# One routed row for all six ranks: layer 0's rows carry six table rows, weights and destinations, and each page finds its own

## The chip, the cores and the metric

The kernel runs on one core of one Trainium2 chip. A core has TensorE (PE, matmuls, with its weight loads shown apart as PEld), VectorE (DVE), ScalarE (ACT), GpSimd (POOL) and SyncE (SP), and 16 DMA engines. DMAs are issued by SP and ACT (plain ones) and by POOL (indirect ones, whose addresses come from a tile of row numbers). The metric is the device time of one execution in microseconds (us). Before the change it was 2058.91 us, the median of 3 runs (2055.96 to 2059.22).

## The reference

The input is x with 128 graphs of 64 nodes and 256 features, so 8192 tokens, and an adjacency matrix for each graph. Two layers follow each other. Each layer is a graph part and a mixture of experts, both added to their input:

```
# layer 0
x = x + graph0(layernorm(x), adj)       # aggregate, 256 -> 1024, rms norm, silu, 1024 -> 256
x = x + experts0(layernorm(x))          # 64 experts of 256 x 256, the 6 best for each token
# layer 1
x = x + graph1(layernorm(x), adj)
x = x + experts1(layernorm(x))          # 8 experts 256 -> 512 -> 256, the 2 best for each token

def experts0(x):
    top, which = top_k(x @ gate_w.T, 6)
    p = softmax(top)                                    # six weights for a token
    y = sum_k p[k] * (x @ lattice_weights[which[k]])    # six products for a token
    return layernorm(x + y @ out_w.T + out_b) * ln_g + ln_b
```

The change is in experts0: how the six copies of a token get to their experts, and how each copy's weight and place of return travel with it.

## The kernel before, in words

The work has four stages, one behind the other.

The block stage of layer 0 (about 0 to 600 us) takes 32 blocks of 256 tokens. A block goes through the graph part, is normalized (`residual_b`, L729), transposed (`turn`, L741), gated (`gate`), and its six best experts are found (`choose`). `count` and `places` work out where each of the six copies of a token goes in a table in DRAM, which has one row for a copy and is filled by expert, so that each 128 rows in it (a page) belong to one expert. `send` (L776, L330) then writes the rows with indirect DMAs on POOL's queue: one for each of two tiles and six ranks of a block, 12 in all, each with 128 rows. `staggered` runs the stages of several blocks side by side with the lags of the list at its end: `place` is 3 blocks behind, the sends of the ranks 2 to 5 are 4 behind.

A row has 258 columns: 256 of the token, one with the destination (token x 6 + rank, an integer in a float's bits), one with the weight. As destination and weight differ between the ranks, the tile xs holds six copies of a block's tokens: ACT writes them with one ACTIVATE of 1536 columns for each of two tiles (L736), `weigh` (L278) writes the destinations, `release` (L303) the weight of one rank before its sends.

The lattice stage (about 613 to 1177 us) first takes 12 early pages, the first page of each of 12 experts, and then 404 pages in 202 pairs (`mean_pages`; more only if the routing needs them, and here it does not). A pair goes through `fetch` (SP reads two pages into a tile px, 22 buffers, asked for 12 pairs ahead), `flip` (PE transposes, ACT copies), and `apply` (L907): PE multiplies each page by its expert's matrix, DVE scales the result by the weight column of px into px itself (L922), and `reply` (L339) writes the 128 results with an indirect DMA on POOL's queue to the rows of `r0.answer` that the destination column of px names. A page table, made by DVE at the end of the block stage (`page_table`, L358), tells which rows and which expert a page has. Rows of a page that no token fills come from a filler tile; its destination is out of range, so that nothing is written for it. During the first 64 pairs ACT also issues a fill of the end of an expert's part of the table.

The graph stage of layer 1 (from 1131 us on, beside the end of the lattice stage) begins with `load_y`, which reads the six products of each token from `r0.answer`. The first five blocks may be read before the last replies land, the others wait for them. The expert stage of layer 1 (about 1530 us to the end) is the same idea with other sizes and is not touched, but shares the class `Router`.

On PE, DVE and ACT the instructions run in the order in which the program writes them (`manual_schedule`). On SP and POOL a planner orders them. All waits are put in by the framework: whoever writes a tile's buffer again waits until those that used the buffer before are done with it. A tile has as many buffers as its `bufs` says, or else its pool; the pool `wx0` of the lattice stage has three:

```
with tc.tile_pool(name="wx0", bufs=3, reuse_waits="tile") as wx, \
...
stages = ((-12, fetch), (0, apply),
          (-2, lambda j: flip(j) if j < 4 else None), (-3, lambda j: flip(j) if j >= 4 else None))
```

The numbers are lags: in step s the kernel writes fetch of pair s+12, apply of pair s, and flip of pair s+3.

Of the kernel before, what the change touches and what calls it, by code (L numbers as in the profile page):

```python
# [78 lines left out]
class Router:  # L79
# [14 lines left out]

    def __init__(self, tc, pool, small, dram, n, D, E, K, T, pg, S, epoch, name, R, total=None, like=None):
        nc = tc.nc
# [9 lines left out]
        self.spare = self.chunks * self.pitch  # L106
        self.W = D + 2
        assert T == 2 and epoch == 4 and n % self.EP == 0 and S % pg == 0 and (5 * T * P <= S or S >= n)
# [30 lines left out]
        nc.gpsimd.memset(self.filler, 0.0)  # L139
        fill_to = self.filler[:, :, D].bitcast(I32)  # L140
        if total is None:
            self.answer = dram.tile([n * K, D], F32, name=name + "y")
            nc.gpsimd.iota(fill_to, pattern=[[0, pg // P]], base=n * K, channel_multiplier=0)
        else:
            nc.gpsimd.iota(fill_to, pattern=[[P, pg // P]], base=n, channel_multiplier=1)
            nc.sync.dma_start(out=total[n:n + pg, :].rearrange("(t p) d -> p t d", p=P), in_=self.filler[:, :, :D])
# [4 lines left out]
    def look(self, m):  # L151
# [10 lines left out]
        v.memset(self.firsts, 0.0)  # L162
        v.tensor_scalar(self.firsts[:, :m], t, float(self.spare), None, op0=ALU.add)
        self.full_pages -= m

# [112 lines left out]
    def weigh(self, b, top, xs):  # L278

        nc, T, K, D, n = self.nc, self.T, self.K, self.D, self.name  # L280
        w = self.small.tile([P, T, K], F32, name=n + "w")
        den = self.small.tile([P, T], F32, name=n + "den")
        nc.vector.tensor_scalar(xs[:, :, :, D].bitcast(I32), self.dest, float(b * T * P * self.each), None,
                                op0=ALU.add)
        nc.vector.tensor_sub(w, top[:, :, :K], top[:, :, 0:1].to_broadcast([P, T, K]))
        nc.scalar.activation(w, w, AF.Exp)
        return w, den
# [9 lines left out]

    def normalize(self, w, den):
        nc = self.nc
        nc.vector.reduce_sum(den, w, axis=AX.X)  # L300
        nc.vector.reciprocal(den, den)

    def release(self, k, w, den, xs):  # L303

        self.nc.vector.tensor_mul(xs[:, :, k, self.D + 1], w[:, :, k], den)

    def places(self, b, hot):

# [13 lines left out]
        prod = self.work.tile([P, T, K, E], F32, name=n + "prod", bufs=1)  # L322
        nc.vector.tensor_mul(prod, hot, place.unsqueeze(2).to_broadcast([P, T, K, E]))
        row = self.small.tile([P, T, K], F32, name=n + "rowf")
        nc.vector.tensor_reduce(row, prod, op=ALU.add, axis=AX.X)
        out = self.small.tile([P, T, K], I32, name=n + "row")
        nc.vector.tensor_copy(out, row)
        return out

    def send(self, row, xs, late, ranks=None, tiles=None):  # L330
        groups = ("late", "send") if late else ("send", "late")
        for t in tiles or range(self.T):
            for k in ranks or range(self.K):
                i = self.nc.gpsimd.indirect_dma_start(  # L334
                    out=self.table[:, :], out_offset=bass.IndirectOffsetOnAxis(ap=row[:, t, k:k + 1], axis=0),
                    in_=xs[:, t, k, :], in_offset=None)
                self.alone(i.ins, *groups)

    def reply(self, i, x, y):  # L339

        d = self.nc.gpsimd.indirect_dma_start(  # L341
            out=self.answer[:, :],
            out_offset=bass.IndirectOffsetOnAxis(ap=x[:, self.D:self.D + 1].bitcast(I32), axis=0),
            in_=y, in_offset=None, bounds_check=self.n * self.K - 1, oob_is_err=False)
# [13 lines left out]
    def page_table(self, scratch):  # L358
# [83 lines left out]
        v.tensor_scalar(self.tab[:, 0, :], row, float(self.spare), None, op0=ALU.add)  # L442
        v.tensor_scalar(self.tab[:, 1, :], exp, float(E - 1), None, op0=ALU.min)

    def fill_end(self, e):
# [49 lines left out]
def two_layer_gnn_moe_kernel(ctx: ExitStack, tc: tile.TileContext, a: dict, out: bass.AP):  # L495
# [83 lines left out]
    xn1_dram = [dram.tile([C, D], F32, name=f"xn1_{b}") for b in range(NB)]  # L579
    r0 = Router(tc, const, small, dram, N, D, E0, K0, T, P, 14 * P, 4, "r0", 3)  # L580
    W = r0.W
    r1 = Router(tc, const, small, dram, N, D, E1, 2, T, 2 * P, N, 4, "r1", 1, total=out, like=r0)

    lat_pool = tc.tile_pool(name="lat", bufs=1)
# [19 lines left out]
    with tc.tile_pool(name="c0", bufs=1) as c0, \  # L604
# [124 lines left out]
        def residual_b(b):  # L729
# [3 lines left out]
            nc.vector.scalar_tensor_tensor(nm, mv[:, :, 0], -1.0, rs, op0=ALU.mult, op1=ALU.mult)  # L733
            B["xs"] = xs = work.tile([P, T, K0, W], F32, name="xs", bufs=3)
            for t in range(T):
                nc.scalar.activation(xs[:, t, :, :D], x1[:, t, :].unsqueeze(1).to_broadcast([P, K0, D]),  # L736
                                     AF.Identity, bias=nm[:, t:t + 1], scale=rs[:, t:t + 1])
            nc.sync.dma_start(out=by_tile(x1_dram[b]), in_=x1)
            nc.sync.dma_start(out=by_tile(xn1_dram[b]), in_=xs[:, :, 0, :D])

        def turn(b):  # L741
            B = blocks[b]
            pt = psum.tile([P, KD, C], F32, name="ps")
            ops.transpose(pt, B["xs"][:, :, 0, :])
            B["xn1T"] = xn1T = work.tile([P, KD, C], F32, name="xn1T", bufs=1)
# [20 lines left out]
        def place(b):  # L766
            B = blocks[b]
            r0.normalize(*B["w"])
            B["row"] = r0.places(b, B["hot"])
            send(b, 0)  # L770
# [5 lines left out]
        def send(b, k):  # L776

            B = blocks[b]
            r0.release(k, *B["w"], B["xs"])
            r0.send(B["row"], B["xs"], b > LOOK, (k,))  # L780
# [55 lines left out]
    with tc.tile_pool(name="e0", bufs=1, reuse_waits="tile") as ex, \  # L836
# [6 lines left out]
        for j in (0, 3, 2, 1, None, 4, 5):  # L843
            if j is None:
                ex.tile([P, 1008], F32, name="space")
            else:
                early[j] = ex.tile([P, 2, W], F32, name=f"early{j}")
        xTs = {}
# [14 lines left out]
        def apply_early(j):  # L863
            py = py_pool.tile([P, 2, D], F32, name="py")
            for q in range(2):
                for k in range(KD):
                    nc.tensor.matmul(py[:, q, :], lhsT=xTs[j][:, k, ts(q, P)], rhs=lat[:, 2 * j + q, k, :],
                                     start=(k == 0), stop=(k == KD - 1))
            for q in range(2):
                px = early[j][:, q, :]  # L870
                nc.vector.tensor_scalar(px[:, :D], py[:, q, :], px[:, D + 1:D + 2], None, op0=ALU.mult)
                r0.reply(0, px, px[:, :D])

# [5 lines left out]
    with tc.tile_pool(name="wx0", bufs=3, reuse_waits="tile") as wx, \  # L879
# [7 lines left out]
        def fetch(j):  # L887
            Q = pairs[j]
            Q["px"] = px = wx.tile([P, 2, W], F32, name="px", bufs=22)
            for q in range(2):  # L890
# [6 lines left out]
        def flip(j):  # L897
# [7 lines left out]
            nc.scalar.copy(xT[:, :, :n * P], pt[:, :, :n * P])  # L905

        def apply(j):  # L907
            Q = pairs[j]
# [12 lines left out]
            for q in range(n):  # L921
                nc.vector.tensor_scalar(px[:, q, :D], py[:, q, :], px[:, q, D + 1:D + 2], None, op0=ALU.mult)  # L922
                r0.reply(2 * j + q, px[:, q, :], px[:, q, :D])


        stages = ((-12, fetch), (0, apply),
                  (-2, lambda j: flip(j) if j < 4 else None), (-3, lambda j: flip(j) if j >= 4 else None))
# [19 lines left out]
    with tc.tile_pool(name="c3", bufs=1, reuse_waits="tile") as c3, \  # L947
# [146 lines left out]
        def residual1_b(b):  # L1094
            B = blocks[b]
            rs, nm = ops.scale_shift(B["mv3"], B["std3"])
            B["xs"] = xs = work.tile([P, T, 2, W], F32, name="xs", bufs=3)
            for t in range(T):
# [72 lines left out]
    with tc.tile_pool(name="pt4", bufs=2, space=PSUM, reuse_waits="tile") as pt_pool, \  # L1171
# [15 lines left out]
        def fetch1(i):  # L1187
            Q = pages[i]
            Q["x"] = x = wx.tile([P, 2, W], F32, name="px", bufs=4)
            if i < 0:  # L1190
# [88 lines left out]
```

## Time and profile before

| | |
|---|---|
| median of 3 runs | 2058.91 us (2055.96 to 2059.22) |
| the profiled execution | 2052.92 us, span of its instructions 2051.1 us |
| granted TensorE clock, mean | 0.974 |
| busy over the span: PE, DVE, POOL, ACT | 1923.0, 1200.0, 1162.0, 1018.1 us |
| POOL's indirect DMAs: sends, early replies, replies | 384, 12, 404 |
| replies, mean of one | 973 ns busy, 123.3 us idle before all of them |
| sends, mean of one | 1047 ns busy |
| HBM | 195 GB/s over the span |

A line of a group has the line of the code, the engine, the operation, the tiles written and read, the shape and the count; then busy us, the mean ns of one, and the idle time of the engine before them with what ended it. A line of the order of time has its start in us, its length, the engine and the line; a bracket at its end tells how long the engine sat idle before it and what it was waiting for. A view of one tile has min/median/max in ns and the first and last start in us. Busy times are shares of a span whose stages have different limits; the stretches of the prediction take them apart.

### The profile page before, as it was taken

The numbers are of one execution on the slowest core, as the hardware profiler recorded it, in microseconds if no ns is written. First come the engines' busy times: TensorE is split into PE (matmuls) and PEld (weight loads), VectorE is DVE, ScalarE is ACT, GpSimd is POOL, SyncE is SP. The second block draws the span as 40 slices with busy tenths as digits, with TensorE's granted clock in tenths as the row PEclk, the third lists the DMA queues.
The fourth block names the chain that finished last, engine by engine and source line by source line (L and its number), as shares of the span: only waits on it lengthen the run. The fifth ranks groups of instructions, "written<-read, shape, count | busy, mean of one in ns | idle before, by whom it ended". The sixth has DMA issues, their size and how long they took to land. (4 is left out here: it accounts for less than half of the span.)

```text
span 2051.1 us, 37214 instructions
## 1 busy us (share of the span) xinstructions
PE 1923.0 (94%) x10516; PEld 1678.1 (82%) x10516; DVE 1200.0 (59%) x4205; ACT 1018.1 (50%) x2033; POOL 1162.0 (57%) x1134
## 2 busy tenths in 40 slices
PE   6999999999966989999999799999989999999996
PEld 5888888888865778888877688888868888888885
DVE  5899999999975333344333389999862222222221
ACT  4888888888851222222222266666643333333332
POOL 1377667677677777777777723333343444444443
PEclk9999999999977999999999899999989999999998
DMA  4244555544476988666665799888527766666664
GB/s 123 80 143 148 168 165 170 169 159 141 133 267 206 309 252 267 214 207 207 207 207 171 266 362 338 267 278 278 190 92 172 178 162 162 162 163 163 163 163 86
DMA packets 282561, 397.91 MB, mean 194 GB/s; under 512 B 56025, under 2 KB 236393, under 8 KB 282353
## 3 DMA queue, kind: packets, MB, share of 16 engines
q1 hardware_dynamic: 202880, 246.61, 40.2%
q0 software_dynamic: 64416, 136.14, 22.1%
q10 hardware_dynamic: 15056, 12.69, 1.9%
q8 instruction: 94, 1.54, 0.3%
q14 instruction: 115, 0.93, 0.2%
HBM read 222.84 MB, written 176.64 MB: 195 GB/s over the span
## 5 line engine op out<-in xcount | busy, mean ns | idle before, releaser
L334 POOL DMA_INDIRECT r0x<-xs,r0row x384 | 402.1, 1047 | 236.0 <-DVE lat L706 72.2
L341 POOL DMA_INDIRECT r0y<-px x404 | 393.3, 973 | 123.3 <-DMA r0y<-px 49.7
L918 PE MATMUL py<-lat,pxT 128*128 x1616 | 389.4, 384 | 18.7 <-ACT pxT L905 15.4
L351 POOL DMA_INDIRECT out_x<-py_s,px x138 | 214.6, 1555 | 293.8 <-DMA out_x<-py_s,px 125.9
L922 DVE TENSOR_SCALAR px<-py,px 128x256 f32<-128x256 f32 x404 | 177.0, 480 | 309.6 <-PE py L918 303.9
L918 PEld LDWEIGHTS py<-lat,pxT 128*128 128x128 f32 x1616 | 294.3, 192 | 59.3 <-ACT pxT L905 20.4
L905 ACT COPY pxT<-pt 128x512 f32<-128x512 f32 x202 | 117.9, 585 | 368.6 <-PE pt L903 252.7
L1217 ACT ACTIVATE phid<-ph,pw 128x256 f32<-128x256 f32 x276 | 130.6, 473 | 323.2 <-issue 213.9
L1215 PE MATMUL ph<-pxT,pw 128*128 128x256 f32 x1104 | 251.3, 381 | 0.7 <-ACT pxT L1206 0.7
L1235 PE MATMUL py<-fw,phid 128*128 (+1 forms) x1104 | 249.7, 379 | 0.0
L717 PE MATMUL ps<-lat 128*128 128x256 f32 x1024 | 238.5, 382 | 0.0
L1215 PEld LDWEIGHTS ph<-pxT,pw 128*128 128x128 f32 x1104 | 210.9, 191 | 30.0 <-ACT pxT L1206 1.1
L684 PE MATMUL ph<-lat 128*128 128x256 f32 x1024 | 232.2, 386 | 2.7 <-DVE lat L706 2.0
L1235 PEld LDWEIGHTS py<-fw,phid 128*128 128x128 f32 x1104 | 204.5, 190 | 25.0
L684 PEld LDWEIGHTS ph<-lat 128*128 128x128 f32 x1024 | 195.1, 193 | 29.4 <-issue 2.4
L334 POOL DMA_INDIRECT r1x<-xs,r1row x128 | 127.7, 998 | 160.9 <-DVE r1run L313 47.0
L717 PEld LDWEIGHTS ps<-lat 128*128 128x128 f32 x1024 | 193.8, 192 | 24.9
L1229 DVE TENSOR_SCALAR p<-p 128x2 f32<-128x2 f32 x69 | 12.8, 186 | 225.5 <-ACT p L1228 225.5
L1238 DVE TENSOR_TENSOR py_s<-py,pb 128x512 f32<-128x512 f32 x69 | 47.7, 692 | 154.9 <-PE py L1235 152.7
L903 PE MATMUL pt<-ident,px 128*128 128x128 f32 x808 | 125.3, 276 | 11.6 <-DMA px<-r0x 11.3
L903 PEld LDWEIGHTS pt<-ident,px 128*128 128x128 f32 x808 | 100.4, 142 | 37.7 <-DMA px<-r0x 8.9
L994 PE MATMUL ps<-ident,y 128*128 128x128 f32 x768 | 94.7, 281 | 16.1 <-DMA y<-r0y 16.1
(303 smaller groups left out, 2980.4 us busy)
## 6 DMA issues: line engine op xcount, KB each, us to landing
px<-r0x SPq DMA_DIRECT2D x404, 129.0 KB
y<-r0y SPq DMA_DIRECT2D x64, 768.0 KB
pw<-in_L_ffn_W1b SPq DMA_DIRECT2D x69, 514.0 KB
px<-r1x SPq DMA_DIRECT2D x69, 258.0 KB
x<-x SPq DMA_DIRECT2D x64, 256.0 KB
pb<-in_L_ffn_b SPq DMA_DIRECT2D x69, 128.0 KB
r0x<-r0filler ACTq DMA_DIRECT2D x64, 129.0 KB
lat<-in_x SPq DMA_DIRECT2D x32, 256.0 KB
```

Source lines behind the costliest of these rows:

```text
L334: i = self.nc.gpsimd.indirect_dma_start(out=self.table[:, :], out_offset=bass.IndirectOffsetOnAxis(ap=row[:, t, k:k + 1], axis=0), in_=xs[ ...
L341: d = self.nc.gpsimd.indirect_dma_start(out=self.answer[:, :], out_offset=bass.IndirectOffsetOnAxis(ap=x[:, self.D:self.D + 1].bitcast(I32 ...
L351: i, d = f"{self.name}add{i}", self.nc.gpsimd.indirect_dma_start(out=self.total[:, :], out_offset=bass.IndirectOffsetOnAxis(ap=x[:, self.D ...
L684: nc.tensor.matmul(ph[:, c, :], lhsT=w1[:, k, ts(2 * j + c, P)], rhs=B["aggT"][:, k, :], start=(k == 0), stop=(k == KD - 1))
L717: nc.tensor.matmul(B["po"][:, t, :], lhsT=B["hT"][:, c, ts(t, P)], rhs=w2[:, c, :], start=False, stop=(t == T - 1 and c == KH - 1))
L903: nc.tensor.transpose(pt[:, k, ts(q, P)], Q["px"][:, q, ts(k, P)], ident)
L905: nc.scalar.copy(xT[:, :, :n * P], pt[:, :, :n * P])
L918: nc.tensor.matmul(py[:, q, :], lhsT=xT[:, k, ts(q, P)], rhs=lat[:, ds(regs["e"][(2 * j + q) % 4], 1), k, :].rearrange("p o d -> p (o d)") ...
L922: nc.vector.tensor_scalar(px[:, q, :D], py[:, q, :], px[:, q, D + 1:D + 2], None, op0=ALU.mult)
L1215: nc.tensor.matmul(ph, lhsT=w[:, k * F1 + c * P:k * F1 + (c + 1) * P], rhs=Q["xT"][:, k, :], start=(k == 0), stop=(k == KD - 1))
L1217: nc.scalar.activation(hid[:, c, :], ph, AF.Relu, bias=w[:, KD * F1 + c:KD * F1 + c + 1], scale=1.0)
L1235: nc.tensor.matmul(py[:, t, :], lhsT=Q["hid"][:, c, ts(t, P)], rhs=fw2[:, ds(e, 1), c, :].rearrange("p o d -> p (o d)"), start=(c == 0), s ...
```

## The change

Each token of a block has one row for all six ranks. The row has 274 columns: 256 of the token, six table rows (where each of the six copies stands), six weights, six destinations. `xs` has one copy of the tokens in place of six and four buffers in place of three; every send of a block reads the same row. `places` writes the six table rows into `xs` as floats, `normalize` writes all six weights at once, and `release` turns one rank's table rows into integers for the send's addresses, where it wrote one rank's weights before.

A page no longer finds a weight and a destination at a fixed column. The new function `own` compares the six table rows of each row of a page with the row's own place in the table, and sums weights and destinations over the one rank where they are equal. It has four DVE instructions for a pair and writes four small tiles, the last of which, `to`, holds the integers that the reply's indirect DMA takes as its addresses. For that a page must know its own rows: `page_table` writes the first rows of all pages to DRAM, and `spread_rows` reads them back to all 128 partitions and adds the partition's number. In the list of stages `own` of pair s+1 is written ahead of `apply` of pair s. px has 20 buffers in place of 22. The early pages call `own` in `apply_early`, with tiles in the pool `et`, which has four buffers.

```diff
-        self.W = D + 2
+        self.W = D + (3 * K if shared else 2)
...
     def page_table(self, scratch):
...
+        if self.shared:
+            v.tensor_scalar(row, row, float(self.spare), None, op0=ALU.add)
+            nc.sync.dma_start(out=self.rows_dram, in_=row)
+
+    def spread_rows(self, pool):
+
+        n = -(-self.pages // 4) * 4
+        out = pool.tile([P, n], F32, name=self.name + "rows", bufs=1)
+        flat = self.rows_dram.rearrange("p j -> (p j)")[:n]
+        self.nc.sync.dma_start(out=out, in_=rows_of(flat))
+        self.nc.vector.tensor_scalar(out, out, self.lane, None, op0=ALU.add)
+        return out
...
     def weigh(self, b, top, xs):
-        nc.vector.tensor_scalar(xs[:, :, :, D].bitcast(I32), self.dest, float(b * T * P * self.each), None,
+        nc.vector.tensor_scalar(xs[:, :, D + 2 * K:], self.dest, float((b * T * P - self.n) * self.each), None,
                                 op0=ALU.add)
...
-    def normalize(self, w, den):
+    def normalize(self, w, den, xs):
...
+        nc.vector.tensor_mul(xs[:, :, D + K:D + 2 * K], w, den.unsqueeze(2).to_broadcast([P, self.T, K]))
+
+    def release(self, k, row, xs):
+
+        self.nc.vector.tensor_copy(row[:, :, k], xs[:, :, self.D + k])
+
+    def own(self, px, rows, small):
+
+        v, D, K = self.nc.vector, self.D, self.K
+        n = px.shape[1]
+        mine = small.tile([P, 2, K], F32, name=self.name + "mine")[:, :n]
+        got = small.tile([P, 2, 2, K], F32, name=self.name + "got")[:, :n]
+        out = small.tile([P, 2, 2], F32, name=self.name + "sum")[:, :n]
+        to = small.tile([P, 2], I32, name=self.name + "to")[:, :n]
+        v.tensor_tensor(mine, px[:, :, D:D + K], rows.unsqueeze(2).to_broadcast([P, n, K]), op=ALU.is_equal)
+        v.tensor_mul(got, px[:, :, D + K:].rearrange("p q (a k) -> p q a k", k=K),
+                     mine.unsqueeze(2).to_broadcast([P, n, 2, K]))
+        v.tensor_reduce(out, got, op=ALU.add, axis=AX.X)
+        v.tensor_scalar(to, out[:, :, 1], float(self.n * K), None, op0=ALU.add)
+        return out[:, :, 0], to
...
     def places(self, b, hot, xs=None):
+        if xs is not None:
+            nc.vector.tensor_reduce(xs[:, :, self.D:self.D + K], prod, op=ALU.add, axis=AX.X)
+            return out
...
-    def reply(self, i, x, y):
+    def reply(self, i, to, y):
-            out_offset=bass.IndirectOffsetOnAxis(ap=x[:, self.D:self.D + 1].bitcast(I32), axis=0),
+            out_offset=bass.IndirectOffsetOnAxis(ap=to, axis=0),
...
-            B["xs"] = xs = work.tile([P, T, K0, W], F32, name="xs", bufs=3)
+            B["xs"] = xs = work.tile([P, T, W0], F32, name="xs", bufs=4)
             for t in range(T):
-                nc.scalar.activation(xs[:, t, :, :D], x1[:, t, :].unsqueeze(1).to_broadcast([P, K0, D]),
-                                     AF.Identity, bias=nm[:, t:t + 1], scale=rs[:, t:t + 1])
+                nc.scalar.activation(xs[:, t, :D], x1[:, t, :], AF.Identity, bias=nm[:, t:t + 1], scale=rs[:, t:t + 1])
...
-            Q["px"] = px = wx.tile([P, 2, W], F32, name="px", bufs=22)
+            Q["px"] = px = wx.tile([P, 2, W0], F32, name="px", bufs=20)
...
+        def own(j):
+            n = min(2, r0.pages - 2 * j)
+            pairs[j]["own"] = r0.own(pairs[j]["px"][:, :n], page_rows[:, 2 * j:2 * j + n], wx)
...
-                nc.vector.tensor_scalar(px[:, q, :D], py[:, q, :], px[:, q, D + 1:D + 2], None, op0=ALU.mult)
-                r0.reply(2 * j + q, px[:, q, :], px[:, q, :D])
-        stages = ((-12, fetch), (0, apply),
+                nc.vector.tensor_scalar(px[:, q, :D], py[:, q, :], Q["own"][0][:, q:q + 1], None, op0=ALU.mult)
+                r0.reply(2 * j + q, Q["own"][1][:, q:q + 1], px[:, q, :D])
+        page_rows = r0.spread_rows(wx)
+        stages = ((-12, fetch), (-1, own), (0, apply),
```

## The prediction, before the change was run

> **What bounds the kernel now.** I read the stretches by engine first, then the reply tile's own instructions, then the order of time at three places. Columns of the stretches: length, busy time of PE, weight load, DVE, ACT, POOL (instructions), granted clock, DMA share, GB/s.
>
> ```profile
> 100.00:550.00 450.00, 440.42 (x2486) 387.04 (x2485) 426.10 (x1438) 380.34 (x728) 316.43 (x302) 1.00 0.47 156
> 590.00:660.00 70.00, 40.36 (x187) 32.50 (x186) 44.07 (x159) 11.91 (x19) 53.84 (x54) 0.73 0.70 228
> 660.00:800.00 140.00, 125.54 (x661) 106.62 (x660) 48.19 (x110) 32.27 (x56) 106.44 (x111) 0.99 0.91 279
> 800.00:1000.00 200.00, 198.82 (x1101) 174.96 (x1101) 80.47 (x184) 53.90 (x93) 152.12 (x157) 1.00 0.70 215
> 1000.00:1130.00 130.00, 121.43 (x623) 100.22 (x621) 45.69 (x105) 29.60 (x51) 98.96 (x102) 0.99 0.63 190
> ```
>
> In the block stage (to about 590) PE is busy 98% and DVE 95%. In the lattice stage (660 to 1130) PE looks like the bound, but POOL only looks free: 0.97 of DMA_INDIRECT plus 0.30 of issue is a 1.275 us beat without a hole, 157 in 200 us. The replies' own rows tell who ends last:
>
> ```profile
> L341 POOL DMA_INDIRECT r0y<-px x404: 967/969/1412, 660.8 to 1176.0; - x135
> L341 POOL DMA_INDIRECT r0y<-early x12: 969/972/992, 645.5 to 659.5; - x12
> ```
>
> 404 replies at 1.275 are 515 us, which is 660.8 to 1176.0: POOL sets the end of this stage, 2.55 us a pair of pages, where an unstalled PE takes 2.17. PE's and DVE's lead over it is stored in the 22 buffers of px:
>
> ```profile
> 1130.09 0.97 POOL L341 DMA_INDIRECT r0y<-px  x1 [0.30 <-DMA r0y<-px]
> 1130.39 0.88 DVE L922 TENSOR_SCALAR px<-py,px 128x256 f32<-128x256 f32 x2 [0.85 <-PE py L918]
> ```
>
> DVE finishes the last pair at 1131.3, POOL 46 us (18 pairs) later. PE spends that time on the next stage. Two stretches show what it gets done:
>
> ```profile
> 1131.00:1152.00 21.00, 8.98 (x46) 8.40 (x47) 0.59 (x4) 0.58 (x1) 15.81 (x18) 0.70 0.92 317
> 1152.00:1190.00 38.00, 34.43 (x217) 30.12 (x216) 25.62 (x91) 19.38 (x42) 20.15 (x22) 0.98 0.72 272
> ```
>
> 21 us are start-up (constants and first loads), then PE is nearly full. Last, what a tile costs that a reply still reads:
>
> ```profile
> 654.44 0.97 POOL L341 DMA_INDIRECT r0y<-early  x1 [0.30 <-DMA px<-r0x]
> ...
> 659.60 1.07 ACT L905 COPY pxT<-pt 128x512 f32<-128x512 f32 x2 [2.99 <-DMA r0y<-early]
> ```
>
> ACT wants memory of a tile that a reply reads, and starts 5.2 us after that reply's issue: the tile is held until the data has landed, not until POOL has issued. The landing records of the 404 replies, counted from the end of POOL's 0.97, have these medians: 3.2 us for the first 120 replies, 1.9 for the next 248 (quartiles 1.6 and 2.3), 4.9 for the last, when the next stage's constants load.
>
> **The change, part by part.** The sum is made on the profiled execution: 2052.9 us (span 2051.1); the median of the timed runs, 2058.9, is 6 higher.
>
> *Routed row without six copies.* Per block ACT writes two times 256 columns in place of 1536:
>
> ```profile
> L736 ACT ACTIVATE xs<-x,bn_nm,rstd x64: 1652/1677/1687, 54.4 to 604.9; 128x1536 f32<-128x1536 f32 x64
> L708 ACT ACTIVATE lat<-lat,c_L_gnn_rms_weight 128x256 f32<-128x256 f32 x211 | 87.1, 494 | 3.5 <-DVE lat L706 3.2
> L76 PE MATMUL ps<-ident,xs 128*128 128x128 f32 x108 | 17.5, 285 | 9.6 <-ACT lat L677 9.6
> ```
>
> 2 x (1.677 - 0.494) = 2.4 us of ACT a block, 76 in all, but beside a PE that is 98% busy. What PE can gain is its wait behind ACT's queue in front of the turn (L76): 9.6 us over 27 blocks. DVE at 95% may keep half. Taken: -5, ends -10 and 0. After 588 POOL sends without a hole until 645, so the shorter ACT chain of the last blocks gains nothing there. The wait for a free xs buffer is 0.2 us in all, so the fourth buffer is worth nothing.
>
> *DVE in the block stage.* weigh, release and places keep their counts; one 12-element product comes in (0.165, as L285), one cast goes (0.173, L327): 0. One operation more in look, one in the page table, and a few constants at the start: under 1 us, beside POOL's sends and the first loads.
>
> *Rows of 1096 bytes in place of 1032.* Sends, fetches and fills move 6% more, 7 MB in all. POOL's issue time does not follow the size (0.969 median for sends and replies), SP issues the same number of fetches, and the fetches are far ahead: 0, but it lengthens landings a little; that is inside the bounds below.
>
> *Page rows.* One store and one spread load on SP behind the page table, whose last operation is at 637.2, then one DVE operation ahead of the first own. The first scale of the stage now is at 655.6, and POOL needs it only at 660.8 (early replies before it). If SP put the store ahead of the six lattice loads that it issues from 571 to 600, 6 MB at 0.3 MB/us would end at 657: still covered to within some 5 us. If the spread load fell behind the first 40 page fetches (58 in 41.6 us, so 29 us after 646.7), scale and POOL would start 16 us late. Taken 0, ends 0 and +16.
>
> *own: the added work.* Four small DVE operations a pair (0.157 to 0.186 each by L300, L285, L1229), 0.66 x 202 = 133 us on an engine that is 40% busy in this stage: hidden as work. POOL's descriptor work can suffer from it: a send takes 1.051 on average beside a DVE busy 95%, a reply 0.973 beside 40%. 25 points more DVE make 0.078 x 25/55 = 0.035 a reply at most in proportion, x 404 = 14; many of the block stage's operations are long, so I take +8, ends 0 and 32 (all 0.078).
>
> The Trainium skill (SBUF — State Buffer, Who interferes with whom) states that a DVE instruction with two SBUF inputs contends with a GpSimd instruction that reads SBUF, the second to issue blocking fully. If each of own's two such products held up a reply for its 0.16 us, that would be 65 us instead of 8; the row of the sends, under a far denser DVE, speaks against it.
>
> *own: the added wait.* This is the term that decides. `to` has three buffers (the pool's default). So own(j+1) writes the tile that reply(j-2) reads, and must wait until it has landed. On DVE own(j+1) stands ahead of the scales of pair j, behind which wait reply(j) on POOL and, four py buffers on, PE's matmuls. DVE loses its lead: two pairs instead of 18. And a loop closes: second reply of j-2 issued, 0.97 + landing L, `to` 0.19, first scale 0.48, POOL's start after DVE 0.27 (L305 ends 551.90, send 552.17), reply(j) issued, 1.275 on to its second. Two pairs then take 3.2 + L, against 5.1 now: it costs as soon as L is over 1.9, the very median of the middle of the stage.
> First 64 pairs, where the fills run too: L 3.2 gives 3.2 a pair, +42; a slower loop moves less, so I take L 2.8, +29. The other 138: only the landings over 1.9 count, about 0.2 a time, 0.1 a pair, +14. Sum +43; ends 0 (L never over 1.9) and +100 (all landings as recorded, the last 16 pairs' too).
>
> The Trainium skill (DMA: Bandwidth & Descriptors, Anatomy of one DMA — SWDGE (gpsimd) path) puts a software DMA's fixed time at about 2 us, most of it the write receipt. An estimate by that page, L 2.0 throughout, would make +10 instead of +43; the records of this trace go above it wherever loads compete.
>
> *The lost lead.* PE's last matmul now comes about 11 us before the last reply, not 46. Then start-up 21 us (with 9 us of work) and the other 34.4 us of work at full rate: PE reaches the state of 1190 (13 us after the last reply now) some 45 us after it. Cost 32; ends 25 (start-up quicker without the replies' traffic) and 46 (the whole lead). The two px buffers fewer cost nothing once the lead is two pairs.
>
> Sum: -5 + 8 + 43 + 32 = +78, so 2131 on the profiled execution and 2137 on the median. I say 2135, its own range 2095 to 2180.
>
> **The rivals.**
> *Held only until issue.* If `to` is free when POOL has read the offsets, the loop is 3.2 us for two pairs and never binds; only the lead goes: -5 + 8 + 32 = +35, about 2091. Against it: ACT's wait above, which is for a landing; for it: that tile held data, not offsets.
> *Faster: the wait does not bind DVE at all.* If the tile is released so that DVE may run ahead as now, own is hidden, POOL's beat and end stay, and the block stage's L76 wait decides: -10 + 0 to +5, about 2052 on the median. It decides only if DVE's lead stays above some 15 pairs. Three buffers speak against it.
> *Landings grow.* If fetches and fills bunch up so that L stays at 4.1 (the 90% point of the first 120 replies), a pair takes 3.65: +1.1 x 202 = 222, with the lead some 2310.
>
> **How the numbers follow.** Forecast 0.72, held until issue 0.11, faster 0.11, landings grow 0.06. Slower is the first, second and fourth. Of the faster case 0.02 lies within 0.2% (4 us, about what a measurement of this kernel tells from none). Below 2070 lie 0.11 of the chance, above 2185 some 0.08; so the range is 2070 to 2185.
>
> **What would show it.** DVE's own line in the lattice stage waits for DMA r0y<-px, some 200 times. POOL's replies show holes and end near 1220 instead of 1177; DVE's last scale is within 6 us of that end. The xs activation falls to about 0.5 us. The share of DMA in the stage falls. The prediction is wrong if POOL's beat stays at 1.275 and DVE still ends 40 us ahead of it, or if the spread load holds up the first pair.

## The result, and the profile after

The changed kernel takes 2184.93 us (median of 4 runs, 2177.05 to 2190.62); the kernel before, beside it, 2059.06 (2055.96 to 2059.88). The ratio is 1.061, with an interval of 1.057 to 1.065: slower by 126 us, where the forecast was slower by 76. The profiled execution took 2188.7 us, with a span of 2186.9; before it was 2051.1, so the two profiles differ by 135.8.

Where the 135.8 lie, from the start times of the same instructions in both traces (all in us from the start; "lead" is the time from the end of DVE's last scale to the end of POOL's last reply; the block period is the mean over the blocks 8 to 28, and replies are counted from start to start):

| | before | after | difference | forecast for this piece |
|---|---|---|---|---|
| block period | 17.93 | 18.29 | +0.36 a block | |
| last send of the block stage | 644.2 | 656.6 | +12.4 | -5 |
| from there to the first reply of a page | 16.6 | 29.8 | +13.2 | 0 (end +16) |
| first to last reply (404) | 515.1 | 585.9 | +70.8 | +43 and +8 |
| lead | 45.8 | 3.9 | | |
| last reply to the end | 875.1 | 914.6 | +39.5 | +32 |

All four pieces grew. I go through them, the lattice stage with its lead first.

**The lattice stage.** Stretches by engine of the kernel after (length, busy time of PE, weight load, DVE, ACT, POOL with instructions, granted clock, DMA share, GB/s):

```profile
100.00:550.00 450.00, 443.96 (x2448) 384.69 (x2448) 427.57 (x1417) 321.19 (x717) 318.23 (x295) 1.00 0.49 158
660.00:800.00 140.00, 109.42 (x523) 90.45 (x524) 57.76 (x246) 25.66 (x44) 78.59 (x82) 0.91 0.77 235
800.00:1000.00 200.00, 162.59 (x826) 135.85 (x825) 95.72 (x414) 39.69 (x68) 132.97 (x138) 0.97 0.68 207
```

Between 800 and 1000 POOL issued 157 indirect DMAs before and 138 now; PE fell from 198.8 to 162.6 us. No engine is full any more: something that is not an engine sets the pace. The waits name it (engine, line, what it waited for: total us, times, longest):

```profile
DVE r0to L331 <- DMA r0y<-px,r0to: 288.1, 166, 4.5
...
POOL r0y L371 <- DVE px L968: 109.1, 140, 8.9
PE py L964 <- DVE r0mine L327: 93.9, 99, 2.9
```

DVE waits 166 times for a reply to land before it may write the next destinations (L331, `to`), POOL waits behind DVE, and PE behind DVE. In the order of time, at the end of the stage (start, duration, engine, line; in brackets the idle time before it and what ended it):

```profile
1267.67 0.17 DVE L331 TENSOR_SCALAR r0to<-r0sum 128x2 int32<-128x2 f32 x1 [2.51 <-DMA r0y<-px,r0to]
1267.75 1.65 DVE L968 TENSOR_SCALAR px<-py,r0sum 128x256 f32<-128x256 f32 x4
1268.50 0.98 POOL L371 DMA_INDIRECT r0y<-px,r0to  x1 [1.73 <-DVE px L968]
...
1272.34 0.97 POOL L371 DMA_INDIRECT r0y<-px,r0to  x1 [0.30 <-issue]
```

The landing ends 2.51 us of idleness on DVE, then come `to`, the scales, and POOL's reply, which had been waiting 1.73 us. The last four replies follow at 1.28 us each. The replies' own rows, and the scales':

```profile
L371 POOL DMA_INDIRECT r0y<-px,r0to x404: 966/969/986, 686.4 to 1272.3; - x135
```

```profile
L968 DVE TENSOR_SCALAR px<-py,r0sum x404: 466/476/484, 685.7 to 1268.9; 128x256 f32<-128x256 f32 x135
```

A reply is as long as before (0.969 median); only the holes between the replies are new. The last scale now starts 3.4 us before the last reply, not 45.

**From the last send to the first reply.** SyncE's queue from 640 to 700, and then the order of time there, after:

```profile
SPq L518 <- DMA r0x<-xs,r0row: 34.2, 4, 30.5
SPq L522 <- DMA r0y<-early,r0to: 9.1, 1, 9.1
```

```profile
656.63 0.97 POOL L364 DMA_INDIRECT r0x<-xs,r0row  x1 [0.30 <-issue]
...
659.30 1.90 SPq L518 DMA_DIRECT2D early<-r0x  x4
...
667.21 0.97 POOL L371 DMA_INDIRECT r0y<-early,r0to  x1 [4.47 <-DVE early L913]
...
676.69 13.27 SPq L522 DMA_DIRECT2D px<-r0x  x22
...
686.42 0.97 POOL L371 DMA_INDIRECT r0y<-px,r0to  x1 [8.91 <-DVE px L968]
```

The same fetches before:

```profile
631.33 1.91 SPq L476 DMA_DIRECT2D early<-r0x  x4
...
646.72 41.57 SPq L480 DMA_DIRECT2D px<-r0x  x58
```

The last four early pages are fetched only once the last sends of the block stage have landed (659.3; before 631.3), and the first page of the main loop only once an early reply has landed (676.7; before 646.7). Neither wait is in the program's logic: the fetch of an early page does not need block 31's `xs`, and the fetch of the first page does not need an early reply. They come from the places of the tiles in memory, as the experiment on them below shows.

**The block stage.** The copies' activation fell as intended, and PE's wait at the turn with it; yet the blocks became longer:

```profile
L76 PE MATMUL ps<-ident,xs 128*128 128x128 f32 x256 | 40.2, 279 | 6.7 <-ACT xs L1146 4.4 <-ACT xs L778 2.3
...
L778 ACT ACTIVATE xs<-x,bn_nm,rstd 128x256 f32<-128x256 f32 x64 | 35.2, 608 | 0.3
```

0.608 us in place of 1.677, twice a block; PE's wait for ACT in front of the turn went from 16.2 (9.6 + 6.6, out of 19.6 for all uses of L76) to 2.3 in the blocks. The pace didn't follow, so ACT was not on the path. DVE's groups between 100 and 550 us have two that are new or longer:

```profile
L317 DVE CAST r0row<-xs 128x2 int32<-128x2 f32 x149 | 28.7, 194 | 0.8
...
L217 DVE CAST r0which<-r0idx 128x12 f32<-128x12 uint32 x25 | 9.6, 386 | 0.9
```

and before, in the same stretch:

```profile
L305 DVE TENSOR_TENSOR xs<-r0w,r0den 128x2 f32<-128x2 f32 x150 | 21.9, 147 | 0.0
...
L207 DVE CAST r0which<-r0idx 128x12 f32<-128x12 uint32 x26 | 4.7, 181 | 0.9
```

The release, which was a product of 0.147 us in this stretch, is a cast of 0.194, and an unchanged cast (L217, before L207 with 0.181) takes 0.386.

### The profile page after: what moved, and what is told of

The parts are those of the page before. It is cut to its first block, busy times and chain, and to the rows that moved or that the text cites. A ratio compares the mean times of both kernels' runs of the same rounds, so it can differ in the third digit from the quotient of the medians.

```text
span 2186.9 us, 38064 instructions
## 1 busy us (share of the span) xinstructions
PE 1961.5 (90%) x10516; PEld 1691.9 (77%) x10516; DVE 1321.1 (60%) x5041; ACT 950.8 (43%) x2033; POOL 1170.2 (54%) x1135
## 5 line engine op out<-in xcount | busy, mean ns | idle before, releaser
L364 POOL DMA_INDIRECT r0x<-xs,r0row x384 | 411.8, 1072 | 238.3 <-DVE lat L748 74.2
L371 POOL DMA_INDIRECT r0y<-px,r0to x404 | 391.8, 970 | 204.0 <-DVE px L968 109.1
L964 PE MATMUL py<-lat,pxT 128*128 x1616 | 403.5, 394 | 99.8 <-DVE r0mine L327 93.9
L964 PEld LDWEIGHTS py<-lat,pxT 128*128 128x128 f32 x1616 | 298.8, 195 | 158.8 <-issue 78.0
L331 DVE TENSOR_SCALAR r0to<-r0sum 128x2 int32<-128x2 f32 x208 | 43.7, 210 | 289.9 <-DMA r0y<-px,r0to 288.1
L968 DVE TENSOR_SCALAR px<-py,r0sum 128x256 f32<-128x256 f32 x404 | 175.4, 476 | 3.7 <-PE py L964 3.7
```

Of the source, the lines that this page charges most:

```text
L364: i = self.nc.gpsimd.indirect_dma_start(out=self.table[:, :], out_offset=bass.IndirectOffsetOnAxis(ap=row[:, t, k:k + 1], axis=0), in_=xs[ ...
L371: d = self.nc.gpsimd.indirect_dma_start(out=self.answer[:, :], out_offset=bass.IndirectOffsetOnAxis(ap=to, axis=0), in_=y, in_offset=None, ...
L964: nc.tensor.matmul(py[:, q, :], lhsT=xT[:, k, ts(q, P)], rhs=lat[:, ds(regs["e"][(2 * j + q) % 4], 1), k, :].rearrange("p o d -> p (o d)") ...
L968: nc.vector.tensor_scalar(px[:, q, :D], py[:, q, :], Q["own"][0][:, q:q + 1], None, op0=ALU.mult)
```

## The experiments

The first theory (A) is the prediction's: the three buffers of `to` make DVE wait for landings, that slows the replies and takes away DVE's lead. For the block stage and the transition the trace after gave new theories: DVE's casts set the block's pace; the tiles' places in memory delay the fetches. to20, to4, onecast and layout ran together. The kernel before took 2056.20 us beside them, 2.9 less than beside the kernel after, so that some 3 us of each difference to 2184.93 below may not be the edit's.

**Twenty buffers of `to`.**

```diff
-    def own(self, px, rows, small):
+    def own(self, px, rows, small, hold=None):
...
-        to = small.tile([P, 2], I32, name=self.name + "to")[:, :n]
+        to = small.tile([P, 2], I32, name=self.name + "to", bufs=hold)[:, :n]
...
+            pairs[j]["own"] = r0.own(pairs[j]["px"][:, :n], page_rows[:, 2 * j:2 * j + n], wx, 20)
```

> The changed kernel with one edit: the tile of reply addresses (to) gets 20 buffers in place of 3. Theory A (the three buffers hold DVE until a reply two pairs back has landed; it stretches the replies from 515 to 586 us and takes away DVE's lead over POOL): POOL's beat is 1.275 us again, first to last reply 515 us, DVE ends some 15 pairs ahead of the last reply, and both costs go: 2185 - 71 - 39 = 2075 us (2065 to 2088). Rival B (own's four operations or the wider rows slow POOL or the fetches, the wait is only where DVE happens to stand): POOL's replies still take 570 us or more and the time stays within 15 us of 2185.

Measured: 2086.53 us, ratio 1.015 (1.013 to 1.017); 98 us of the 126 are gone. The wait of L331 for a landing is not among this kernel's waits any more. Its replies, its scales, and its stretch from 800 to 1000:

```profile
L371 POOL DMA_INDIRECT r0y<-px,r0to x404: 967/970/1368, 684.0 to 1201.1; - x135
```

```profile
L968 DVE TENSOR_SCALAR px<-py,r0sum x404: 473/480/487, 683.3 to 1161.9; 128x256 f32<-128x256 f32 x135
```

```profile
800.00:1000.00 200.00, 195.84 (x1076) 171.21 (x1075) 135.94 (x537) 53.15 (x91) 152.34 (x157) 1.00 0.75 228
```

517.0 us from first to last reply, 157 replies in the 200 us again, and DVE 39.7 us ahead at the end. DVE does all of own's work beside it (135.9 us busy in place of 80.5), and POOL's replies are not longer (0.970 median): in this stage own's work is hidden, and only its wait cost.

**Four buffers of `to`.** The same edit with 4 in place of 20: the wait stays, one pair later.

> The changed kernel with 4 buffers of the tile of reply addresses in place of 3. Theory A: the loop of own, scale and reply now spans three pairs, 3.2 us + landing against 7.65, so it binds only for landings over 4.4 us: first to last reply about 520 us. But DVE may still run only three pairs ahead, so the next stage still starts late: 2185 - 65 = 2120 us (2110 to 2130), which prices the loop and the lost lead apart. If the loop and the lead were one thing, a fourth buffer would give back a third or so of both, about 2150. Rival B: 2185.

Measured: 2117.21 us, ratio 1.030 (1.028 to 1.032).

```profile
DVE r0to L331 <- DMA r0y<-px,r0to: 211.0, 146, 4.3
```

```profile
L371 POOL DMA_INDIRECT r0y<-px,r0to x404: 967/970/986, 684.4 to 1200.4; - x135
```

```profile
L968 DVE TENSOR_SCALAR px<-py,r0sum x404: 466/476/487, 683.6 to 1196.7; 128x256 f32<-128x256 f32 x135
```

DVE still waits 211 us for landings, and yet the replies take 516.0 us: with one more pair of room the wait ends before POOL needs the result. The lead is still lost (4.2 us). So the two halves of theory A come apart: after to to4 is the loop, 68 us (2184.9 - 2117.2; between the two profiles the replies differ by 70); to4 to to20 is the lead, 31 us (2117.2 - 2086.5).

**One cast of twelve in place of six of two.** `places` turns all six table rows into integers at once, ahead of the sends.

```diff
     def places(self, b, hot, xs=None):
...
             nc.vector.tensor_reduce(xs[:, :, self.D:self.D + K], prod, op=ALU.add, axis=AX.X)
+            nc.vector.tensor_copy(out, xs[:, :, self.D:self.D + K])
             return out
...
-            r0.release(k, B["row"], B["xs"])
             r0.send(B["row"], B["xs"], b > LOOK, (k,))
```

> The changed kernel, but the six table rows of a block become integers in one operation in places, in place of one operation for each rank before its sends; nothing is left out. Theory D (DVE sets the pace of the block stage, the new casts at 0.19 us in place of products at 0.147 lengthen a block from 17.9 to 18.3 us): six operations at 0.19 less and one at 0.17 more take about 1 us a block, the last send comes about 25 to 30 us earlier, the time is about 2157 us (2150 to 2168). Rival E (PE, busy 98 to 99% there, sets the pace): a block stays within 0.1 us of 18.3 and the time within 6 us of 2185.

Measured: 2160.97 us, ratio 1.051 (1.049 to 1.053); the block period is 17.72, below that of the kernel before. In DVE's groups between 100 and 550 the other cast is short again:

```profile
L217 DVE CAST r0which<-r0idx 128x12 f32<-128x12 uint32 x26 | 4.6, 177 | 0.9
L354 DVE CAST r0row<-xs 128x12 int32<-128x12 f32 x25 | 4.3, 172 | 0.9
```

and PE's stretch is nearly full, 447.1 of 450 us (after 444.0, before 440.4). DVE set the pace of the blocks, not PE; what ACT was spared shows only when DVE is spared too. The period fell less than the 17.3 expected; with PE busy 447.1 of 450 us, PE is the likely next bound.

**The release by an addition.** The copy becomes an addition of zeros, to see whether the operation or its number costs.

```diff
-        self.nc.vector.tensor_copy(row[:, :, k], xs[:, :, self.D + k])
+        self.nc.vector.tensor_add(row[:, :, k], xs[:, :, self.D + k], self.zero[:, :self.T])
```

It ran first on another chip, where all is slower (the kernel before takes 2304.25 us there), so that its block period can't be set beside the others':

> The changed kernel, but release makes each rank's integers by adding a tile of zeros (a product-like operation on two tiles, the form that release had before the change) in place of a cast; same count, nothing left out. Theory D1 (the cast itself, 0.19 us on average in place of 0.147, lengthens the block): the six cost 0.88 us a block as before the change, a block takes some 18.0 us in place of 18.3, the last send comes some 9 us earlier (about 647), the time is about 2176 us. Rival D2 (where the six stand and what they read makes them long, or another part of the change, such as the product of all six weights, slows the block): they stay over 1.1 us a block, the block at 18.2 to 18.3 and the time at 2185.

Measured there: 2333.35 us, ratio 1.012 (1.006 to 1.018), block period 21.5: neither theory can be read from it. It was run again beside the kernel after, on a chip where the kernel before takes 2057.07:

> The release converts the row numbers by an addition of zeros in place of a copy, six a block; everything else as the kernel after. Theory D1: the copy's own duration (0.19 against 0.15 of the product that stood there before) is what makes the blocks slower: block period 17.9 to 18.05, last send 8 to 10 us earlier than the kernel after, ratio to the kernel after 0.995. Theory D2: any operation there costs the same: period 18.2 to 18.35, ratio to the kernel after 0.999 to 1.001.

> The kernel after itself, so that the two kernels beside it have it on their own chip. Expected at a ratio of 1.057 to 1.065 to the kernel before, block period 18.3, 404 replies in 580 to 590 us, a lead of 4 us.

Measured: the kernel after 2180.83 us (ratio 1.060, 1.059 to 1.062), replies in 581.4 us, lead 3.9; the addition 2174.41 us (ratio 1.057, 1.056 to 1.059), block period 17.97, last send at 648.1 (kernel after there: 656.5). By the period and the last send that is D1: six operations of the same size, only of another kind, give back 0.32 of the 0.36 us a block. The ratio to the kernel after, 0.997, lies between what the two theories gave. Of the 8.4 us by which the last send comes earlier, the whole time keeps 6.4. Why a cast costs more than an addition is in the order of time. The kernel after, DVE and POOL about one send:

```profile
300.94 0.97 POOL L364 DMA_INDIRECT r0x<-xs,r0row  x1 [0.30 <-issue]
301.49 0.39 DVE L317 CAST r0row<-xs 128x2 int32<-128x2 f32 x1
301.56 0.38 DVE L214 MAX8 r0top<-rms_p 128x8 f32<-128x64 f32 x1
...
302.21 0.96 POOL L364 DMA_INDIRECT r0x<-xs,r0row  x1 [0.30 <-DVE r0top L214]
...
302.78 0.37 DVE L217 CAST r0which<-r0idx 128x12 f32<-128x12 uint32 x1
```

and the kernel with the addition, the same place:

```profile
296.88 0.97 POOL L364 DMA_INDIRECT r0x<-xs,r0row  x1 [0.30 <-issue]
297.42 0.15 DVE L317 TENSOR_TENSOR r0row<-xs,r0zero 128x2 int32<-128x2 f32 x1
297.49 0.22 DVE L214 MAX8 r0top<-rms_p 128x8 f32<-128x64 f32 x1
...
298.15 0.97 POOL L364 DMA_INDIRECT r0x<-xs,r0row  x1 [0.30 <-issue]
...
298.55 0.17 DVE L217 CAST r0which<-r0idx 128x12 f32<-128x12 uint32 x1
```

The cast that starts 0.55 us after the send's start ends 0.94 after it; the addition at 0.54 is done in 0.15. Over all sends from 100 to 550 us: of the 149 release casts 25 start between 0.5 and 0.76 us after a send's start, last 0.30 to 0.41, and all end 0.93 to 0.95 after it; the 124 others last 0.13 to 0.17. Of the 150 additions 25 start in the same window, and last 0.15. The held cast delays the MAX8 behind it and shifts the other cast (L217), which before started at 0.47 to 0.49 and passed (23 of 25), into the window as well: 25 of 25 are held, 0.386 on average. That is about 0.24 + 0.21 us a block on the engine that sets the pace.

**The tiles' places.** The addresses that the two compiled kernels give their tiles (bytes in a partition) are:

```
                         before                        after
xs of a block            12384 long, 3 buffers         2192 long, 4 buffers
  block 30               180576                        184960
  block 31 (the last)    205344                        182752
early4, early5           183104, 185184                183584, 185792
page rows                none                          180960, 1792 long
first px                 180992                        182752
```

Before, the last two early tiles and the first px lay over the `xs` of block 30. Now early4 lies over that of block 31, whose sends are the last to land, and over that of block 30. And the new tile of page rows ends at 182752, so that the first px tile comes to lie over early4, which a reply still reads. The run layout moves both apart, with a tile of 8 KB a partition that nobody uses, and by giving out the first px tile before the page rows:

```diff
+            if b == 0:
+                work.tile([P, 2048], F32, name="pad", bufs=1)
             B["xs"] = xs = work.tile([P, T, W0], F32, name="xs", bufs=4)
...
+        px0 = [wx.tile([P, 2, W0], F32, name="px", bufs=20)]
...
-            Q["px"] = px = wx.tile([P, 2, W0], F32, name="px", bufs=20)
+            Q["px"] = px = px0.pop() if px0 else wx.tile([P, 2, W0], F32, name="px", bufs=20)
```

> The changed kernel with other places in memory only: an unused tile of 8 KB a partition ahead of xs, so that the last two early pairs no longer lie on buffers of xs that the last block's sends read, and the tile of page rows behind px, so that the first px buffer no longer lies on an early pair. Theory F (SP holds the last four early fetches until the last send has landed, and the first page fetch until an early reply has; 5 and 9 us of POOL's time between the early and the first reply go there): the last early fetches are issued before 635 us in place of 659, POOL has no hole between its last send and its first reply, the first reply comes at 673 in place of 686, the time is about 2172 us (2165 to 2178). Rival G (the first reply is set by the last send and by DVE's order): the fetches move but the first reply does not, 2185.

Measured: 2162.27 us, ratio 1.051 (1.050 to 1.053).

```profile
616.76 9.27 SPq L518 DMA_DIRECT2D early<-r0x  x12
...
657.85 31.78 SPq L522 DMA_DIRECT2D px<-r0x  x44
```

The early fetches are all issued from 616.8 on, without a stop, and the first reply starts at 671.5, 16.8 us after the last send (before 16.6, after 29.8). The first page is fetched at 657.9, while the early replies still run. The first reply is 14.9 us earlier than in the kernel after, where 13 were expected. The total is below the range given (2165 to 2178), because 10 more come from the replies (575.9 from first to last), which nobody expected. Such a loop differs between runs: the kernel after itself shows 585.9 and 581.4.

**All three.** Twenty buffers, one cast and the tiles moved. On the slower chip:

> The changed kernel with all three edits: 20 buffers of the reply addresses, one cast a block, and the two moved places in memory. If the three costs are apart from each other, the gains measured one at a time add: 2185 - 98 - 24 - 23 = 2040 us (2033 to 2048), below the kernel before (2056). Piece by piece: a block 17.7 us, last send 639, first reply 655 to 656, 404 replies in 516 us to 1171, and 877 us from there to the end, a span of 2048 by that sum. If the gains overlap (the earlier start of the replies lost to POOL or to loads), it ends between 2050 and 2065.

Measured there: 2370.11 us against 2304.25, ratio 1.028 (1.025 to 1.032), with replies in 621 us and a lead of 3.9: between 900 and 1100 us PE runs there at a granted clock of 0.92 and is busy 158.3 of 200 us, DVE waits for PE or for what the profile does not name, no longer for a landing, and the kernel can't be compared with the rest. On this chip it is even slower than the kernel with the addition alone (2333.35), its last send coming at 800 in place of 750; no run here shows why. On the chip of after_again:

> The three edits together once more (20 buffers of `to`, one cast of twelve row numbers per block in place of six releases, the tiles laid out so that no fetch waits for a send or an early reply), beside the kernel before and the kernel after on the same chip. If the three causes are separate, as the single edits say, the kernel after loses 98 (`to`), 24 (casts) and 23 (tiles): 2185 - 145 = 2040 where the kernel before takes 2056 to 2059, that is a ratio of 0.992 (0.988 to 0.997), a block period of 17.7 us, first reply within 15 us after the last early reply, 404 replies in 516 us, a lead of 38 to 42 us. If they overlap (POOL's beat of 1.275 takes over again once two are gone, or DVE's own work costs POOL something when it runs ahead), the ratio is at 1.000 to 1.010.

Measured: 2057.82 us against 2057.07, ratio 1.000 (0.999 to 1.001). On this chip the changed kernel with these three edits is as fast as the kernel before, and not faster: of the two cases expected it is the one in which the savings overlap.

```profile
L372 POOL DMA_INDIRECT r0y<-px,r0to x404: 967/970/1377, 656.1 to 1171.0; - x135
```

```profile
L971 DVE TENSOR_SCALAR px<-py,r0sum x404: 473/481/487, 652.6 to 1132.1; 128x256 f32<-128x256 f32 x135
```

```profile
100.00:550.00 450.00, 447.13 (x2523) 395.18 (x2522) 422.82 (x1333) 329.12 (x738) 325.30 (x305) 1.00 0.50 163
800.00:1000.00 200.00, 196.93 (x1079) 171.46 (x1079) 136.51 (x539) 53.03 (x91) 152.18 (x157) 1.00 0.73 220
```

By pieces it has what the single edits promised: block period 17.72, last send at 639.4, first reply 16.7 later, replies in 514.9, lead 39.5. But the single savings add up to more than the three save together: 145 us against 127 as plain differences, 138 against 126 if each is set against the kernel before that ran beside it. A good part of the gap lies in the replies: the single edits of the block stage and of the places were seen with a loop that waited for landings and happened to run 6 and 10 us shorter; once POOL's beat of 1.275 sets the loop it can't be shorter than 515. After the last reply the profiled run of this kernel, the longest of its 12, needs 889.1 us against 880.0 of to20; that part I can't attribute.

## Why the prediction was right or wrong

The direction and the deciding wait were right, the total was 50 us short. That 2184.93 still lies inside the range, 0.07 us from its upper end, is luck: the wait was priced 28 us too low, and two pieces that were put at nothing or at a gain cost 12 and 13 us. The steps that failed are the halving of the late landings, the block stage with PE as its bound, and the places of the tiles, which the sum left out. By its steps:

*"own: the added wait."* Right in kind: the tile is held until the landing, DVE waits 166 times (some 200 forecast), the lead falls to 3.9 (forecast within 6), the DMA share of the stage falls (0.91 to 0.77 and 0.70 to 0.68). The rivals fall with it: held only until issue and not binding at all by the 166 waits, landings growing by the landing records, whose medians got shorter (2.46 us for the first 128 replies after the change, 1.89 for the next 240, 1.37 for the last). The size was wrong: +71 for +43, and it failed in "Two pairs then take 3.2 + L" read as an average, so that of what a landing takes over 1.9 only half counts for a pair ("about 0.2 a time, 0.1 a pair, +14"; the +29 is halved in the same way). The replies are issued in order, so a late landing moves the next pair as well, and nothing gives it back. The landings recorded in the trace after show what that is worth. Let the second reply of a pair start 2.55 us after that of the pair before it, or 3.2 + L after that of two pairs before, whichever is later: with the recorded L this gives 580 us from the second reply of the first pair to that of the last, and 585 were measured. That is +67 for the measured +71. The same landings give +43 if each excess over 1.9 is halved, as the prediction did, and +87 if it counts in full. So the loop and its 3.2 were right, and so, added up, were the landings; only the averaging was wrong. The first 64 pairs had 3.12 us for the 3.0 taken (+37 for +29), the middle 120 had 2.83 for 2.55 (+34, where +14 was taken for these and the last 18), the last 18 lost next to nothing. In the rival "held only until issue", +35 gives 2094 on the median and not 2091; nothing rests on it.

*"own: the added work."* +8 was too much, the measured term is 0: a reply takes 0.970 on average, before 0.973, with 808 DVE instructions more beside them, and 0.972 and 0.973 in to20 and all3b, where DVE runs ahead again. The rule on two SBUF inputs that the prediction cites from the Trainium skill (SBUF — State Buffer, Who interferes with whom), by which the sum would have had 65 in this place, doesn't show either.

*"The lost lead."* +32, measured +39.5. 29 to 31 of it is the lead alone (to4 against to20, by profile and by median). Another 5 lie between to20 and the kernel before (880.0 and 875.1). They may be the two px buffers fewer, which the prediction put at nothing "once the lead is two pairs": with the lead back, 20 buffers hold 39.7 us and 22 held 45.8. But all3b, with the same 20 buffers and a lead of 39.5, needs 889.1, so that no run shows it. The last 5, between to4 and after, stay open too; the two profiles of the kernel after differ by 2 there (914.6 and 912.7).

*"Routed row without six copies", "DVE in the block stage".* -5 and 0 were wrong; the stage got 12.4 us longer. The prediction read PE at 98% as the bound and let DVE at 95% take only half of the gain. onecast shows that it was the other way round. And it counted the releases as unchanged because their number is: a cast for a product, 0.147 to 0.194, and the cast behind it, 0.181 to 0.386. The sign of this could have been seen in the trace before: the group of that cast had a median of 0.173 and a maximum of 0.401.

```profile
L207 DVE CAST r0which<-r0idx x32: 172/173/401, 65.0 to 611.3; 128x12 f32<-128x12 uint32 x32
```

Two of the casts between 100 and 550 us in that trace start 0.6 and 0.7 us after a send, and end at 0.94, as all held ones do.

*The Trainium skill.* SBUF — State Buffer, Who interferes with whom, was read for the wrong one of its rules. It says too that copies and casts with both sides in SBUF can take the pair of ports that DVE shares with GpSimd, and that the later of the two then blocks. This is the one that fits what the runs show: casts that started 0.5 to 0.76 us into a send were held in 25 of 25 cases, additions with two inputs in none of 25. The runs narrow it: no cast that started before 0.49 us of a send was held, so that a lock, if this is what held them, lay on a part of the send and not on all of it. In DMA: Bandwidth & Descriptors, Anatomy of one DMA — SWDGE (gpsimd) path, the fixed 2 us agree with the middle landings (1.89) and not with the first (2.46), and a sum by it had +10 where 71 were measured: with a margin of 1.9 it is the spread that costs, not the median.

*"Page rows" and the fourth xs buffer.* Taken as 0, the transition got 13.2 longer, near the end of +16 that was given, but not for its reason. The spread load of the page rows was issued at 666.3, ahead of the first page fetch, and was not what that waited for. What was late were the fetches, because tiles whose size changed came to lie over others. The prediction looked at each tile's number of buffers, and not at what lies in the same bytes before it.

*"Rows of 1096 bytes."* 0, as forecast: sends of 0.969 median, and in to20 and all3b the replies in 517 and 515 us.

## What to carry to other kernels

A tile that an indirect DMA reads its offsets from was busy here until the data had landed; give such a tile as many buffers as the engine that writes it is meant to run ahead, for a fourth buffer bought back the pace but not the lead. Where the margin of a wait is near the median of what it waits for, don't cost it by an average: an engine that issues in order never gives a late one back, so play the loop through with the recorded times, one after the other. When tiles change their size or a new one is allocated, look at which tiles now share bytes, and in a stage with two engines near full, cost the change of each operation's kind and place on both, not only their number.

## What the runs showed of the hardware

A DVE cast from SBUF to SBUF that starts 0.5 to 0.76 us after an indirect DMA's start on POOL is held until 0.93 to 0.95 us after it, whatever its size (2 or 12 elements a partition); outside that window it takes its 0.13 to 0.17. The single-input offset addition of own (L331) is held in the same way: 40 of 180 in to20 between 700 and 1130 us start in the window, 0.31 on average, and the others last 0.17. Products, additions and reductions at the same place take their usual 0.15 to 0.19, and none of those in the window is held.

The landings of replies, all of one size, have within one stage a lower quartile of 1.3 us and a 90% point of 4.0 (the second replies of the last 18 pairs). And the same kernel before took 2304 us on one chip, at a mean granted clock of 0.94 to 0.95, and 2056 to 2059 on the others, at 0.97 to 0.98.
